# Float32r parts for every second channel's column transform in all batches, with more of the v product on ScalarE

## The chip, the cores and the metric

The kernel runs on one core of a Trainium2 chip. The metric is the device time of one execution in microseconds (us). The kernel before takes 3088.14 us, the median of three runs (3085.73 to 3089.94). Five engines work side by side, each through its own queue in order: TensorE (PE; its weight loads are listed as PEld), VectorE (DVE), ScalarE (ACT), GpSimd (POOL) and SyncE (SP, which here only issues transfers). [...]

## The reference, cut to what matters

The input `x` has 4 batches of 64 channels of 256 x 256 float32. Four layers follow each other.

Layers 0, 1 and 3 are long convolutions. A small network of sines makes two filters of 256 values per channel, `hx` and `hy`; the two-dimensional filter is their outer product, so that the convolution separates into one along the rows and one along the columns. The reference does it with an FFT of twice the length and adds `x * bias`:

```python
y = irfft2(rfft2(x, s=(512, 512)) * rfft2(k, s=(512, 512)) / 512)[..., :256, :256]
out = y + x * bias[:, None, None]
```

Layer 2 works in a Haar wavelet basis:

```python
f1 = haar2d(x)
for i in range(2):
    f4 = einsum('bchw,oc->bohw', f1 * v[i], conv_w[i])
    acc += sign(f4) * relu(abs(f4) - tau[i])
y = haar2d(acc, inverse=True)
return y + x
```

The channels are mixed by a 64 x 64 matrix per coefficient place; `v` and `tau` depend on the place alone, so the kernel mixes first and multiplies by `v` afterwards.

## The kernel before, in words

**Filters.** The networks of the three convolution layers run first, on small tiles. Their filters go to DRAM (`pads`) padded with zeros, and `toeplitz` (line 158) reads a filter back as a 128 x 256 Toeplitz tile per axis. The products of `v` and of `tau` with fixed factors go to DRAM as `scales`, `GT` groups to a tile.

**Convolutions, forward part.** `convolutions(b, ticks, in_parts)` takes the 64 channels of one batch through five stages, one tick apart: `load` (x and a Toeplitz tile), `first` and `second` of layer 0, `first` and `second` of layer 1. Each of the four products is a `contract` (lines 167 and 168): for each half of the columns a product of 256 columns and one of 128. ACT copies the result of a `first` out of PSUM (`a`, L176); DVE evicts a `second` with `y = res * bias + product` (L189). The last stage, `pairs`, also does the first Haar level along the rows into a ring `sd` of 8 channels (L230, L231) and stores it to `keep`. Every four channels `levels` does the other row levels on DVE (L240, L241).

Then `down` does the Haar transform along the columns, one product of the 128 x 128 Haar matrix with 512 columns. It has two forms. The plain one (L263) multiplies float32 by float32. The other, used where `in_parts` is set, has `split` ahead of it: ACT rounds the tile to float32r (`w[:, 0]`, L251), DVE forms the remainder (`w[:, 1]`, L252), and `down` adds two float32r products in PSUM (L259). Before the change only batch 0 goes in parts. ACT copies the coefficients out (`co`, L267) and SP stores them to `coef` in DRAM.

**Mixing.** `mixing(b, start, n_act)` takes 64 groups, each 4 coefficient rows of all 64 channels. `load` brings a group's coefficients, and at every `GT`-th group a tile `vt` of scales. `mix` multiplies by the mixing matrix: four products of 256 columns into `px` (L308), a PSUM tile of two banks with two buffers. The product with `v` is shared: DVE does the first `16 - n_act` of 16 slices of 64 in one instruction (L325), ACT does the other `n_act` with one instruction each (L327), into the tile `f4`. In the order of the queues L327 stands behind L325's semaphore. `shrink` forms |f4| on ACT (L333) and its sign on ACT (L334), and DVE takes tau off (L335); `signed` multiplies (L340) and `add` sums the two terms into the result `z` in SBUF (L344). `n_act` is 8 in batches 0 to 2 and 6 in the last one.

**Inverse and the last convolution.** `inverse(b)` takes each channel of `z` through the inverse transforms (`pw`, L368 and L369; `pu`, L381), adds the residual, and goes on with layer 3 (`first`, `second` and the store). In batches 0 to 2 every third channel is put off: it is stored to `late`, and `convolution` does its layer 3 during the last batch's mixing.

**What sets the order.** Each stage is registered as an event with a tick and a place in the tick (`at`, `stream`), and the sorted list of events is the program's order. Channels of batch b + 1 are spread over the ticks in which batch b is mixed, some 0.8 to 0.9 channels a tick. From this order the framework makes one instruction queue for each engine; it also moves instructions within some distance, so that neighbours on an engine can change places. Buffers come from tags with a fixed number of buffers: `in` (x and the put-off channels, 4), `toep` (5), `f4` (2, shared by the v products, the inverse's parts and the split's parts), `vt` (2), and four PSUM banks `mm` for all products but `px`. A tile waits until the oldest tile of its tag has been read for the last time.

Of the kernel before, what the change touches and what calls it, by code (L numbers as in the profile page):

```python
# [9 lines left out]
F32 = mybir.dt.float32  # L10
F32R = mybir.dt.float32r
# [5 lines left out]
B, C, S, EMB, ORD = 4, 64, 256, 33, 64  # L17
P = 128
ROW = S + P

GT = 8
BUFS = {"res": 1, "y": 3, "co": 2}

INV_2PI = float(np.float32(1.0 / (2.0 * math.pi)))
# [13 lines left out]
def conv_seq_kernel(ctx, tc, x, fz, fw, bias, decay, haar, haar_row, factors, vt, taut, wmix, out):  # L38
# [37 lines left out]
    with tc.tile_pool(name="filt", bufs=2) as fp, tc.tile_pool(name="fps", bufs=4, space=PSUM) as fps:  # L76
# [12 lines left out]
        for layer in range(3):  # L89
            z = fp.tile([EMB, S + 2 * ORD], F32, name=f"z{layer}", tag="z", bufs=3)  # L90
            nc.sync.dma_start(z, fz[layer])
            w = fp.tile([ORD, 2, 3 * ORD + 4], F32, name=f"w{layer}", tag="w", bufs=3)
# [5 lines left out]
        for step in range(3):  # L98
            for layer, axis in both:
                z, w = zs[layer], ws[layer]  # L100
# [8 lines left out]
                u = fp.tile([ORD, S], F32, name=f"u{step}_{layer}_{axis}", tag="u", bufs=3)  # L109
# [102 lines left out]
                if stage is not None:  # L212
                    at(tick + s, -s, stage, unit)

    def convolutions(b, ticks, in_parts=False):

        st = {}

        def load(c):
            xt = io.tile([P, 2, S], F32, name=f"x_{b}_{c}", tag="in", bufs=4)  # L220
            nc.sync.dma_start(xt, x[b, c].rearrange("(k p) w -> p k w", p=P))
            st[c] = {"x": xt, 0: toeplitz(0, c, f"t0_{b}_{c}")}

        last_second = second(b, st, "a1", 1, "y0", "y1", "res")

        def pairs(c):
            last_second(c)
            v = st.pop(c)["y1"].rearrange("p k (w e) -> p k w e", e=2)
            t = sd[:, c % 8]
            nc.vector.tensor_add(t[:, :, 0, :], v[:, :, :, 0], v[:, :, :, 1])  # L230
            nc.vector.tensor_sub(t[:, :, 1, :], v[:, :, :, 0], v[:, :, :, 1])  # L231
            nc.scalar.dma_start(keep[b][c], t)

        def levels(steps):
            def run(n):
                t = sd[:, n % 2 * 4 : n % 2 * 4 + 4]
                for step in steps:
                    v = t[:, :, :, 0, :].rearrange("p c k (w e) -> p (c k) w e", e=2 * step)
                    even, odd = v[:, :, :, 0], v[:, :, :, step]
                    nc.vector.tensor_sub(odd, even, odd)  # L240
                    nc.vector.scalar_tensor_tensor(even, even, 2.0, odd, ALU.mult, ALU.subtract)  # L241

            return run

        parts = {}

        def split(c):

            w = parts[c] = mx.tile([P, 2, 2, S], F32R, name=f"sp_{b}_{c}", tag="f4")
            t = sd[:, c % 8].rearrange("p k e w -> p k (e w)")  # L250
            nc.scalar.copy(w[:, 0], t)  # L251
            nc.vector.tensor_tensor(w[:, 1], t, w[:, 0].bitcast(F32), ALU.subtract)  # L252

        def down(c):
            ps = bank(f"pz_{b}_{c}")
            flat = "p k w -> p (k w)"
            if in_parts:
                for i in range(2):
                    nc.tensor.matmul(  # L259
                        ps.rearrange(flat), hbr, parts[c][:, i].rearrange(flat), start=(i == 0), stop=(i == 1)  # L260
                    )
            else:
                nc.tensor.matmul(  # L263
                    ps.rearrange(flat), hbt, sd[:, c % 8].rearrange("p k e w -> p (k e w)"), start=True, stop=True
                )
            t = io.tile([P, 2, S], F32, name=f"co_{b}_{c}", tag="co", bufs=BUFS["co"])
            nc.scalar.copy(t, ps)  # L267
            nc.sync.dma_start(coef[b][:, c].rearrange("k p w -> p k w"), t)

        stream(  # L270
            [load, first(b, st, "x", 0, "a0"), second(b, st, "a0", 0, "x", "y0", "y", ahead=1), first(b, st, "y0", 1, "a1"), pairs],
            ticks,
        )
        for n in range(C // 4):
            end = ticks[4 * n + 3] + 4
            for s, steps in enumerate([(1,), (2, 4), (8, 16, 32, 64)]):
                at(end + 1 + s, 1, levels(steps), n)
            for j in range(4):
                if in_parts:
                    at(end + 3 + j, 2, split, 4 * n + j)  # L280
                at(end + 4 + j, 2, down, 4 * n + j)
        return ticks[-1] + 11

    def mixing(b, start, n_act):

        st = {}

        def load(g):
            f = mx.tile([P, 2, S], F32, name=f"f_{b}_{g}", tag="f", bufs=3)
            nc.sync.dma_start(f, coef[b].rearrange("k c p w -> (k c) p w")[:, 2 * g : 2 * g + 2])  # L290
            st[g] = {"f": f}
            if g % GT == 0:
                t = mx.tile([P, 2, GT, 16], F32, name=f"vt_{b}_{g}", tag="vt")
                nc.sync.dma_start(t, scales[g // GT])
                st["vt", g // GT] = t

        def scale(g, i):
            return st["vt", g // GT][:, i, g % GT, :]

        def over(g, i, n):  # L300
            return scale(g, i)[:, :n].unsqueeze(2).to_broadcast([P, n, C])

        def mix(g):
            f = st[g]["f"]
            ps = psx.tile([P, 2, 2, S], F32, name=f"px_{b}_{g}", tag="mix")
            for q in range(2):
                for h in range(2):
                    nc.tensor.matmul(  # L308
                        ps[:, h, q, :],
                        f[:, q, h * P : (h + 1) * P],  # L310
                        wb.rearrange("p r n -> p (r n)"),
                        start=True,
                        stop=True,
                    )
            if g == 0:

                one, two = ps[:, :, 0, :P], ps[:, :, 0, P:]
                d = mx.tile([P, 2, P], F32, name=f"d_{b}", tag="mag")
                nc.vector.tensor_copy(d, two)
                nc.vector.tensor_sub(two, one, d)  # L320
                nc.vector.tensor_add(one, one, d)
            f4 = mx.tile([P, 16, C], F32, name=f"f4_{b}_{g}", tag="f4")
            px = ps.rearrange("p h q (r i o) -> p (h q r i) o", r=2, i=2)
            n = 16 - n_act
            nc.vector.tensor_tensor(f4[:, :n], px[:, :n], over(g, 0, n), ALU.mult)  # L325
            for j in range(n, 16):
                nc.scalar.mul(f4[:, j], px[:, j], scale(g, 0)[:, j : j + 1])  # L327
            st[g]["f4"] = f4

        def shrink(g):  # L330
            f4 = st[g]["f4"]
            mag = mx.tile([P, 16, C], F32, name=f"mag_{b}_{g}", tag="mag")
            nc.scalar.activation(mag, f4, AF.Abs)  # L333
            nc.scalar.activation(f4, f4, AF.Sign)  # L334
            nc.vector.tensor_sub(mag, mag, over(g, 1, 16))  # L335
            st[g]["mag"] = mag

        def signed(g):
            mag = st[g]["mag"]
            nc.vector.scalar_tensor_tensor(mag, mag, 0.0, st[g]["f4"], ALU.max, ALU.mult)  # L340

        def add(g):
            parts = st.pop(g)["mag"].rearrange("p (h r i) o -> p h r i o", h=2, i=2)
            nc.vector.tensor_add(z[:, :, 4 * g : 4 * g + 4, :], parts[:, :, :, 0, :], parts[:, :, :, 1, :])  # L344

        for g in range(S // 4):
            at(start + g - 2, 0, load, g)
            for s, stage in enumerate([mix, shrink, signed, add]):
                at(start + g + s, -1 - s, stage, g)
# [61 lines left out]
    def convolution(which, ticks):  # L411

        for (b, c), tick in zip(which, ticks):
            st = {}

            def load(c, b=b, st=st):
                u = io.tile([P, 2, S], F32, name=f"v_{b}_{c}", tag="in", bufs=4)
                nc.sync.dma_start(u, late[b, c])
                st[c] = {"u": u, 2: toeplitz(2, c, f"t2_{b}_{c}")}

            for s, stage in enumerate([load, *last(b, st)]):
                at(tick + s, -s, stage, c)


    def spread(begin, end, n=C):
        return [begin + i * (end - begin - 1) // (n - 1) for i in range(n)]
# [1 line left out]

    put_off = range(2, C, 3)
    groups = S // 4  # L430
    ready = convolutions(0, range(C), in_parts=True)
    ahead = C
    start = ready + 3
    for b in range(B):
        mixing(b, start, 8 if b + 1 < B else 6)
        end = start + groups + 3
        if b + 1 < B:
            ready = convolutions(b + 1, spread(ahead, end + 2))
        else:
            convolution(  # L440
                [(i, c) for i in range(B - 1) for c in sorted(put_off)], spread(start - 2, end + 2, (B - 1) * len(put_off))
            )
        inverse(b, end, put_off if b + 1 < B else ())

        start = max(end + C, ready + 3)
        ahead = start - 3
# [112 lines left out]
```

## Time and profile before

| | before |
|---|---|
| time, median of 3 | 3088.14 us |
| span of the profiled execution | 3090.0 us |
| TensorE granted clock | 0.999 |
| HBM traffic | 209 GB/s over the span |

The share of busy time by slice (40 slices of 77 us; a digit is tenths, 9 is 90% or more) shows the stages. DVE and ACT are fuller where a batch is mixed, slices 6 to 11, 15 to 20, 24 to 29 and 33 to 36:

```profile
PE   5999999999999999999999999999999999999999
DVE  6667677999987878888886879888886889998776
ACT  1333336777765656667665656666774667887554
```

In the tables of groups the columns are the line, the engine and operation, what is written and read, the shapes and the number of instructions; then the busy time in us and the mean duration of one in ns; then how long the engine stood idle just before them and whom it waited for. Where instructions of a kind overlap at their ends, the busy time is less than the number times the mean. In the table of waits the columns are the waiting line, the line that released it, the total in us, how often, and the longest. A timeline row has the start, the length, the engine, the line, and how many instructions were merged into it. A float32 product shows as two instructions.

### The profile page before, as it was taken

How to read it: one execution, taken by the hardware profiler on the slowest of the kernel's cores; microseconds unless marked ns; L12 is line 12 of the kernel's file. 1: busy time of each engine (PE TensorE's matmuls, PEld its weight loads, DVE VectorE, ACT ScalarE, POOL GpSimd, SP SyncE). 2: the span in 40 equal slices, each digit the busy share in tenths (PEclk: the TensorE clock that was granted, in tenths of full speed). 3: DMA queues.
4: the chain of work that ended last, by engine and by line, in shares of the span. 5: the costliest groups of instructions: out<-in, count | busy, mean ns of one | idle time of the engine just before them, and what ended most of it. 6: DMA issues, size and time to landing. Idle time of an engine off the chain costs nothing. (4 is left out here: it accounts for less than half of the span.)

```text
span 3090.0 us, 50474 instructions
## 1 busy us (share of the span) xinstructions
PE 3004.4 (97%) x16944; PEld 2615.3 (85%) x16944; DVE 2523.4 (82%) x4453; ACT 1926.9 (62%) x4054; POOL 0.2 (0%) x4
## 2 busy tenths in 40 slices
PE   5999999999999999999999999999999999999999
PEld 3999988888888888888887888888887888888998
DVE  6667677999987878888886879888886889998776
ACT  1333336777765656667665656666774667887554
POOL 0000000000000000000000000000000000000000
PEclk9999999999999999999999999999999999999999
DMA  4777877666667876666667776666667777877676
GB/s 118 217 230 230 234 227 211 196 193 197 195 193 228 238 223 196 195 207 199 194 205 216 236 229 196 199 195 204 198 195 218 235 238 228 236 233 212 210 211 188
DMA packets 555573, 649.26 MB, mean 210 GB/s; under 512 B 39761, under 2 KB 440500, under 8 KB 555188
## 3 DMA queue, kind: packets, MB, share of 16 engines
q1 hardware_dynamic: 439316, 493.18, 56.5%
q10 hardware_dynamic: 116000, 152.87, 13.7%
q8 instruction: 136, 2.23, 0.3%
q14 instruction: 121, 0.99, 0.1%
HBM read 426.40 MB, written 219.48 MB: 209 GB/s over the span
## 5 line engine op out<-in xcount | busy, mean ns | idle before, releaser
L167 PE MATMUL py<-t,a 128*128 128x256 f32 x3072 | 926.0, 383 | 27.9 <-ACT a L176 24.6
L176 ACT COPY a<-pa 128x512 f32<-128x512 f32 x768 | 458.7, 597 | 466.3 <-PE pa L168 330.7
L168 PEld LDWEIGHTS py<-t,a 128*128 128x128 f32 x3072 | 584.1, 190 | 79.4
L327 ACT ACTIVATE f<-px,vt 128x64 f32<-128x64 f32 x1920 | 422.0, 329 | 352.7 <-DVE f L325 348.3
L167 PEld LDWEIGHTS py<-t,a 128*128 128x128 f32 x3072 | 488.4, 191 | 126.1 <-issue 63.2
L168 PE MATMUL py<-t,a 128*128 128x128 f32 x3072 | 590.6, 274 | 0.0
L308 PE MATMUL px<-wb,f 128*128 128x256 f32 x2048 | 494.2, 380 | 4.3 <-ACT f L327 4.3
L308 PEld LDWEIGHTS px<-wb,f 128*128 128x128 f32 x2048 | 366.0, 191 | 44.1 <-ACT f L327 6.7
L335 DVE TENSOR_TENSOR mag<-mag,vt 128x1024 f32<-128x1024 f32 x256 | 312.2, 1219 | 36.0 <-ACT mag L333 34.8
L167 PE MATMUL pa<-t,x 128*128 128x256 f32 x1024 | 307.5, 382 | 9.4 <-DMA t<-pad 9.3
L340 DVE SCALAR_TENSOR_TENSOR mag<-mag,f 128x1024 f32<-128x1024 f32 x256 | 311.4, 1216 | 0.3
L167 PE MATMUL pa<-t,y 128*128 128x256 f32 x1024 | 306.3, 381 | 1.2 <-DVE y L189 0.9
L333 ACT ACTIVATE mag<-f 128x1024 f32<-128x1024 f32 x256 | 283.9, 1109 | 12.6 <-DVE z L344 6.8
L361 ACT COPY zc<-z 128x512 f32<-128x512 f32 x256 | 281.9, 1102 | 3.9 <-DVE z L199 2.6
L371 ACT CAST w<-pw 128x512 fp32r<-128x512 f32 x256 | 150.2, 587 | 212.3 <-PE pw L369 201.3
L334 ACT ACTIVATE f<-f 128x1024 f32<-128x1024 f32 x256 | 272.0, 1062 | 9.7 <-DVE sd L231 2.4
L189 DVE SCALAR_TENSOR_TENSOR y<-y,bsb,py 128x512 f32<-128x512 f32 x256 | 190.1, 743 | 104.5 <-PE py L168 103.7
L385 DVE SCALAR_TENSOR_TENSOR t<-r,pu 128x512 f32<-128x512 f32 x256 | 175.3, 685 | 86.6 <-PE pu L381 79.6
L189 DVE SCALAR_TENSOR_TENSOR y<-x,bsb,py 128x512 f32<-128x512 f32 x256 | 190.1, 743 | 62.6 <-PE py L168 54.0
L167 PE MATMUL pa<-t,u 128*128 128x256 f32 x772 | 234.1, 385 | 1.1 <-DVE y L189 0.7
L189 DVE SCALAR_TENSOR_TENSOR y<-u,bsb,py 128x512 f32<-128x512 f32 x193 | 143.8, 745 | 102.4 <-PE py L168 98.7
L168 PEld LDWEIGHTS pa<-t,x 128*128 128x128 f32 x1024 | 195.7, 191 | 26.9
(65 smaller groups left out, 4370.7 us busy)
## 6 DMA issues: line engine op xcount, KB each, us to landing
t<-pad SPq DMA_DIRECT2D x768, 256.0 KB, 3.9
x<-in_x SPq DMA_DIRECT2D x256, 256.0 KB, 3.9
keep<-sd ACTq DMA_DIRECT2D x256, 256.0 KB, 3.3
coef<-co SPq DMA_DIRECT2D x256, 256.0 KB, 3.1
f<-coef SPq DMA_DIRECT2D x256, 256.0 KB, 3.9
r<-keep SPq DMA_DIRECT2D x256, 256.0 KB, 3.4
out_y<-y ACTq DMA_DIRECT2D x256, 256.0 KB, 3.6
late<-u ACTq DMA_DIRECT2D x63, 256.0 KB, 2.6
```

What stands on the lines that cost most here:

```text
L167: nc.tensor.matmul(ps[:, m, :], src[:, 0, m * P : (m + 1) * P], t[:, ::-1], start=True, stop=False)
L168: nc.tensor.matmul(ps[:, m, P:], src[:, 1, m * P : (m + 1) * P], t[:, : P - 1 : -1], start=False, stop=True)
L176: nc.scalar.copy(a, ps)
L189: nc.vector.scalar_tensor_tensor(y, s[res], bsb[:, layer, c : c + 1], ps, ALU.mult, ALU.add)
L308: nc.tensor.matmul(ps[:, h, q, :], f[:, q, h * P : (h + 1) * P], wb.rearrange("p r n -> p (r n)"), start=True, stop=True,)
L327: nc.scalar.mul(f4[:, j], px[:, j], scale(g, 0)[:, j : j + 1])
L333: nc.scalar.activation(mag, f4, AF.Abs)
L334: nc.scalar.activation(f4, f4, AF.Sign)
L335: nc.vector.tensor_sub(mag, mag, over(g, 1, 16))
L340: nc.vector.scalar_tensor_tensor(mag, mag, 0.0, st[g]["f4"], ALU.max, ALU.mult)
L361: nc.scalar.copy(a, z[:, :, :, c].rearrange("p h (i k) -> p h k i", k=2))
L385: nc.vector.scalar_tensor_tensor(t, st[c]["r"], 0.5, ps, ALU.mult, ALU.add)
```

## The change

It does three things together, and makes room for them.

- `down` in two float32r parts for every even channel of batches 1 to 3, as well as for all channels of batch 0. It is for PE[...]. `in_parts` becomes the set of channels.
- In the mixings of batches 0 to 2 ACT takes 12 of the 16 slices of the v product (8 before), DVE 4. It is for DVE, which has the remainders to form.
- The parts get a tag of their own, `sp`, with one buffer of 4 KB per partition, where they used the two buffers of `f4`, which the mixing needs.
- For the room, `in` goes from 4 to 3 buffers (2 KB less), and `GT` from 8 to 4 groups per tile of scales (1 KB less; twice as many loads of half the size).

```diff
-GT = 8
+GT = 4
...
-    def convolutions(b, ticks, in_parts=False):
+    def convolutions(b, ticks, in_parts=()):
...
-            xt = io.tile([P, 2, S], F32, name=f"x_{b}_{c}", tag="in", bufs=4)
+            xt = io.tile([P, 2, S], F32, name=f"x_{b}_{c}", tag="in", bufs=3)
...
-            w = parts[c] = mx.tile([P, 2, 2, S], F32R, name=f"sp_{b}_{c}", tag="f4")
+            w = parts[c] = mx.tile([P, 2, 2, S], F32R, name=f"sp_{b}_{c}", tag="sp", bufs=1)
...
-            if in_parts:
+            if c in in_parts:
                 for i in range(2):
                     nc.tensor.matmul(
                         ps.rearrange(flat), hbr, parts[c][:, i].rearrange(flat), start=(i == 0), stop=(i == 1)
...
-                if in_parts:
+                if 4 * n + j in in_parts:
                     at(end + 3 + j, 2, split, 4 * n + j)
...
-                u = io.tile([P, 2, S], F32, name=f"v_{b}_{c}", tag="in", bufs=4)
+                u = io.tile([P, 2, S], F32, name=f"v_{b}_{c}", tag="in", bufs=3)
...
-    ready = convolutions(0, range(C), in_parts=True)
+    ready = convolutions(0, range(C), in_parts=range(C))
...
-        mixing(b, start, 8 if b + 1 < B else 6)
+        mixing(b, start, 12 if b + 1 < B else 6)
...
-            ready = convolutions(b + 1, spread(ahead, end + 2))
+            ready = convolutions(b + 1, spread(ahead, end + 2), in_parts=range(0, C, 2))
```

## The prediction

> **What bounds the kernel now.** I read the page first: busy shares, then each engine's share by time.
>
> ```profile
> span 3090.0 us, 50474 instructions
> PE 3004.4 (97%) x16944; PEld 2615.3 (85%) x16944; DVE 2523.4 (82%) x4453; ACT 1926.9 (62%) x4054; POOL 0.2 (0%) x4
> ```
>
> TensorE (PE) leads, but a kernel with stages is read stage by stage. The three mixings that the change touches run from the first to the last `px` product: 479.7 to 901.3, 1142.3 to 1601.4, 1848.5 to 2309.4 us. The fourth, 2552.3 to 2825.4, keeps its 6 products on ScalarE (ACT). The table of stretches gives them in another order, after the two middle ones:
>
> ```profile
> 1142.30:1601.40 459.10, 452.71 (x2429) 389.67 (x2428) 403.50 (x669) 317.12 (x793) 0.00 (x0) 1.00 0.67 199
> 1848.50:2309.40 460.90, 454.15 (x2430) 390.05 (x2429) 403.43 (x669) 316.97 (x793) 0.00 (x0) 1.00 0.67 198
> 479.70:901.30 421.60, 414.60 (x2178) 352.95 (x2177) 382.26 (x628) 308.40 (x777) 0.00 (x0) 1.00 0.65 195
> 2552.30:2825.40 273.10, 268.10 (x1435) 235.62 (x1435) 265.31 (x310) 233.97 (x553) 0.00 (x0) 1.00 0.79 231
> ```
>
> Columns: length, busy PE, PEld, DVE, ACT, POOL, clock, DMA. One group takes length/63: 7.29, 7.32, 6.69 and 4.33 us. In the second mixing PE is busy 98.6%, VectorE (DVE) 88%, ACT 69%. The fourth shows PE at 98% beside DVE at 97% and ACT at 86%, so neighbours that full need not slow PE.
>
> PE's own work must be counted from start-to-start times, because ends are modelled. The timeline of PE around one `down` of each kind:
>
> ```profile
> 1306.74 0.38 PE L168 MATMUL pa<-t,x 128*128 128x128 f32 x2
> 1306.96 1.02 PE L263 MATMUL pz<-sd,hbt 128*128 128x512 f32 x2
> 1307.82 0.59 PE L167 MATMUL py<-t,a 128*128 128x256 f32 x2
> ```
> ```profile
> 203.43 0.39 PE L168 MATMUL pa<-t,x 128*128 128x128 f32 x2
> 203.56 0.71 PE L259 MATMUL pz<-sp,hbr 128*128 128x512 f32 x2
> 204.11 0.59 PE L167 MATMUL py<-t,a 128*128 128x256 f32 x2
> ```
>
> From the preceding L168 to the following L167 is 1.08 us with the float32 `down`, 0.68 us with the parts: 0.40 us apart. The first form alone occupies 0.86 us (1306.96 to 1307.82), so the second counts 0.46. In the same way a `contract` takes 1.31 us (two L167 and two L168 rows, 1305.65 to 1306.96) and a group's `px` 1.73 us (1303.92 to 1305.65). In the second mixing 57 channels x 4 contracts x 1.31 + 49 downs x 0.86 + 63 x 1.73 = 299 + 42 + 109 = 450 us of 459; in the first (49 channels) 257 + 42 + 109 = 408 of 422. So PE is short of its own sum by 2 to 3% there. What takes that is the hand-over between ACT and DVE; ACT's waits in 1142 to 1602 us:
>
> ```profile
> ACT f L327 <- DVE f L325: 115.7, 57, 3.5
> ACT a L176 <- PE py L168: 8.6, 4, 4.2
> ```
>
> ACT stands 115.7 us behind DVE's share of the product. Per group there is a loop: Abs (L333, ACT), minus tau (L335, DVE), often a y eviction (L189) and the shrink product (L340), then DVE's v product (L325), ACT's v products (L327), copies, Abs of the next group. With start-to-start times 1.17, 1.16, 0.68 x 48/63, 1.16 x 41/63, 0.68, 8 x 0.20 = 1.60 plus one to two copies of 0.47 it is about as long as PE's tick. Following both queues row by row with such times gives 6.7 and 7.3 us a group, the 6.69 and 7.29 measured. Two limits lie close together: PE at 6.5 and 7.1 us, the loop at 6.7 and 7.3.
>
> [...] 8 products run in 1.75 us, 0.20 to start-to-start. [...] the trace has 684 and, for the 256-column copy out of `px` (L319), 417.
>
> **The change part by part.** The rows used:
>
> ```profile
> L327 ACT ACTIVATE f<-px,vt 128x64 f32<-128x64 f32 x1920 | 422.0, 329 | 352.7 <-DVE f L325 348.3 <-DMA keep<-sd 4.1
> L263 PE MATMUL pz<-sd,hbt 128*128 128x512 f32 x384 | 197.7, 597 | 9.1 <-DVE sd L241 7.7 <-DVE w L372 1.4
> L325 DVE TENSOR_TENSOR f<-px,vt 128x512 f32<-128x512 f32 x192 | 131.2, 684 | 1.2
> L252 DVE TENSOR_TENSOR sp<-sd,sp 128x512 fp32r<-128x512 f32 x64 | 44.1, 689 | 57.5 <-ACT sp L251 56.0 <-PE py L168 1.4
> L251 ACT CAST sp<-sd 128x512 fp32r<-128x512 f32 x64 | 40.3, 631 | 2.2 <-DVE sd L241 2.2
> ```
>
> PE: 3 batches x 32 channels leave the float32 form, 96 x 0.40 = 38.4 us less. Of these about 73 lie in mixings (half of the 49 downs in each), 29.4 us; 23 lie in the stretches between, 9.0 us.
>
> ACT: 192 groups x 4 more products x 0.20 = +154 us, and 96 split copies x 0.47 (start to start, as L176) = +45 us. Per group +0.80 and +0.18: in the second mixing from 317/63 = 5.03 to 6.0 us of a tick near 7.1, 85%.
>
> DVE: L325 falls from 512 to 256 columns, 684 to about 417 ns (bounds 0.36, its start-to-start, and 0.42): 192 x 0.27 = -51 us. The 96 subtractions add 96 x 0.63 = +60 us. DVE stays at 6.4 us a group, 90%.
>
> The loop: the products add 0.80, L325 gives back 0.26. With the old order of the queues that would be +0.54 a group. But the instruction order of the changed kernel differs: DVE's next v product stands ahead of the shrink product in 42 of 63 pairs (22 before) in the second and third mixing, in 58 (43) in the first; the y eviction stands between L335 and L325 in 29 (48) and 15 (35). That takes 0.37 + 0.21 off in the second mixing, 0.28 + 0.22 in the first: the tally is level, -0.04 and +0.04. Copies that move into ACT's wait take off more: the row-by-row sum gives 6.55 and 7.2 us, 0.15 and 0.10 less than before. I take this, below PE's 29.4: 63 x (0.15 + 0.10 + 0.10) = 22 us.
>
> The split ahead of a `down`: at the end of each of three conversions PE waited 2 to 3.4 us in L263 for the Haar levels (L241). There the two halves now follow the levels, 0.6 + 0.6 us, 3 times: +3.6 us. Elsewhere the split runs a tick ahead, hidden by the other four contracts.
>
> `sp` gets one own buffer instead of two of `f4`. In batch 0 the split of channel c+1 then follows the `down` of c in ACT's queue, behind the copy L267 that waits for the same product: no new wait, and the result is due a tick (5.7 us) later. Cost zero, hidden by the contracts.
>
> `in` with 3 buffers: x loads of batch 0 go out as the fourth last is freed, 15 to 16 us before use; v loads of the last mixing 11.5 to 15 us before. One buffer less takes one tick, 5.7 and 4.3 us. At least 7 us stay for a landing of 3.9 to 4.1 us: zero, unless DVE lags. `GT` 4: 32 more loads of half the size on SP, two ticks ahead; zero.
>
> Sum: -22 - 9.0 + 3.6 = -27, so 3061 us.
>
> **The rivals.**
> 1. PE gets all of it: 3088 - 38 = 3050 us. For it: PE 98% busy, DVE and ACT both fuller in the fourth mixing. Against it: the loop explains the measured period better than PE's sum.
> 2. Slower: PE's queue stalls at `px`. In the changed order 81 groups' `px` wait for ACT to free the bank (57 before), some directly behind the previous `px`, with the contracts queued behind. The wait before was 0.8 us at most and 4.3 in all; a whole block of products is 12 x 0.20 = 2.4. With 24 (the added ones) to 63 (all that lie in the three mixings) stalls of 1.2 us, half a block, +29 to +76 on 3061: 3090 to 3137. If the loop rose by the +0.54 of the old order in place of falling, 189 x 0.54 - 5 = +97, 3185. For it: ACT's spare time in a group falls from 2.2 to 1.1 us while its waits persist. Against it: the fourth mixing.
> 3. No change: mixings stay pinned by the loop, only the stretches between gain, 3088 - 9 + 3.6 = 3083 us.
>
> **How the numbers follow.** Forecast (3053 to 3072) 0.45, rival 1 (below) 0.15, rival 3 and its neighbourhood (3072 to 3094) 0.22, rival 2 (beyond) 0.18. Range 3045 to 3094: below it lies more than PE can give, above it rival 2. Within 0.2% (3082 to 3094) 0.12; faster 0.45 + 0.15 + 0.10 = 0.70; slower 0.18.
>
> **What would show it.** Right: L263 x192 and L259 x320 instructions; groups in the three mixings near 6.55 and 7.2 us; ACT near 2120 us in all, DVE near 2530; ACT still waiting on L325, but under 1.2 us a group; the fourth mixing unchanged at 273 us. Wrong: `px` waiting for L327 by tens of us, `pa` waiting for loads of x or v, or the loop longer because L334 now stands behind the first product of the next group (8 to 20 of 63 pairs, 1 or none before), so that ACT idles through L335 and L325.

## The result, and the profile after

The changed kernel takes 3049.98 us (median of 4 runs, 3042.65 to 3052.63) against 3086.93 us for the kernel before in the same comparison: ratio 0.9877, 95% interval 0.9857 to 0.9897. That is 37 us less, where 27 were forecast. The time, 3050 us, lies just below the forecast's 3053 to 3072 and is that of rival 1.

The page of the changed kernel, busy shares:

```profile
span 3050.6 us, 51749 instructions
PE 2971.9 (97%) x16944; PEld 2615.0 (86%) x16944; DVE 2518.7 (83%) x4549; ACT 2117.0 (69%) x4918; POOL 0.2 (0%) x4
```

TensorE (PE) lost 32.5 us of modelled busy time, VectorE (DVE) is level (2519, 2530 forecast) and ScalarE (ACT) went from 1927 to 2117 (2120 forecast). The added loads of the engines are as worked out. The stretches from the first to the last `px`, columns as before:

```profile
481.10:890.50 409.40, 403.51 (x2180) 350.55 (x2179) 375.81 (x650) 367.04 (x1052) 0.00 (x0) 1.00 0.67 202
1131.80:1577.80 446.00, 443.42 (x2421) 388.13 (x2420) 395.59 (x690) 373.90 (x1068) 0.00 (x0) 1.00 0.68 204
1823.20:2268.80 445.60, 443.42 (x2421) 388.16 (x2420) 395.56 (x690) 373.95 (x1068) 0.00 (x0) 1.00 0.68 204
2513.60:2785.90 272.30, 267.69 (x1436) 235.73 (x1435) 265.20 (x310) 233.95 (x553) 0.00 (x0) 1.00 0.79 232
```

| stretch | before | after | difference |
|---|---|---|---|
| mixing 1 | 421.6 | 409.4 | -12.2 |
| mixing 2 | 459.1 | 446.0 | -13.1 |
| mixing 3 | 460.9 | 445.6 | -15.3 |
| mixing 4 | 273.1 | 272.3 | -0.8 |
| between 1 and 2, 2 and 3, 3 and 4 | 241.0, 247.1, 242.9 | 241.3, 245.4, 244.8 | +0.3, -1.7, +1.9 |

So the three mixings gave 40.6 us, and the stretches between them nothing. The stretches do not hold quite the same work: in the second and third mixing one `contract` of PE has moved behind the last `px` (2421 PE instructions where there were 2429 and 2430). With its 1.31 us put back, the mixings gave 38.0 us and the stretches between them 2.1. A group takes 6.50, 7.08 and 7.07 us. Of the 40.6 us, 31.1 are PE's busy time (1321.5 to 1290.4 in the three; 2.6 of it are the two contracts) and 9.5 are PE idle time (20.1 to 10.7). In the second mixing of the changed kernel ACT waits for this:

```profile
ACT f L327 <- DVE f L325: 34.8, 32, 4.5
ACT a L176 <- PE pa L168: 26.1, 12, 2.7
```

Its wait for DVE's share of the product fell from 115.7 us to 34.8, while its busy time rose from 317 to 374. Idle time of ACT was filled; what that was worth by itself, the experiments show. Rows of the changed kernel's groups:

```profile
L327 ACT ACTIVATE f<-px,vt 128x64 f32<-128x64 f32 x2688 | 585.0, 348 | 103.2 <-DVE f L325 102.7
...
L259 PE MATMUL pz<-sp,hbr 128*128 128x512 f32 x320 | 116.1, 442 | 9.5 <-ACT sp L251 9.5
...
L252 DVE TENSOR_TENSOR sp<-sd,sp 128x512 fp32r<-128x512 f32 x160 | 109.8, 686 | 68.2 <-ACT sp L251 68.2
...
L325 DVE TENSOR_TENSOR f<-px,vt 128x256 f32<-128x256 f32 x192 | 80.4, 419 | 5.8 <-PE px L308 5.3
```

L325 with 256 columns takes 419 ns (417 taken), L252 686 ns, and the 768 added products cost 163 us of busy time (154 estimated).

### The profile page after: what moved, and what is told of

Same layout as the page of the kernel before. It is cut to its first block, busy times and chain, and to the rows that moved or that the text cites. A ratio compares the mean times of both kernels' runs of the same rounds, so it can differ in the third digit from the quotient of the medians.

```text
span 3050.6 us, 51749 instructions
## 1 busy us (share of the span) xinstructions
PE 2971.9 (97%) x16944; PEld 2615.0 (86%) x16944; DVE 2518.7 (83%) x4549; ACT 2117.0 (69%) x4918; POOL 0.2 (0%) x4
## 5 line engine op out<-in xcount | busy, mean ns | idle before, releaser
L167 PE MATMUL py<-t,a 128*128 128x256 f32 x3072 | 924.5, 383 | 16.6 <-ACT a L176 11.1
L176 ACT COPY a<-pa 128x512 f32<-128x512 f32 x768 | 475.5, 621 | 464.5 <-PE pa L168 352.9
L327 ACT ACTIVATE f<-px,vt 128x64 f32<-128x64 f32 x2688 | 585.0, 348 | 103.2 <-DVE f L325 102.7
L168 PEld LDWEIGHTS py<-t,a 128*128 128x128 f32 x3072 | 584.0, 190 | 79.5
L168 PE MATMUL py<-t,a 128*128 128x128 f32 x3072 | 590.5, 274 | 0.0
L167 PEld LDWEIGHTS py<-t,a 128*128 128x128 f32 x3072 | 491.0, 191 | 89.7 <-issue 32.8
L335 DVE TENSOR_TENSOR mag<-mag,vt 128x1024 f32<-128x1024 f32 x256 | 312.5, 1221 | 52.8 <-ACT mag L333 51.8
L167 PE MATMUL pa<-t,x 128*128 128x256 f32 x1024 | 307.5, 382 | 9.8 <-DMA t<-pad 9.8
L340 DVE SCALAR_TENSOR_TENSOR mag<-mag,f 128x1024 f32<-128x1024 f32 x256 | 312.0, 1219 | 1.1
L167 PE MATMUL pa<-t,y 128*128 128x256 f32 x1024 | 306.6, 381 | 1.3 <-DVE y L189 1.1
L334 ACT ACTIVATE f<-f 128x1024 f32<-128x1024 f32 x256 | 278.7, 1088 | 27.0 <-DVE sd L231 15.6
L167 PE MATMUL pa<-t,u 128*128 128x256 f32 x772 | 236.2, 388 | 2.1 <-DVE u L389 1.4
L168 PEld LDWEIGHTS pa<-t,x 128*128 128x128 f32 x1024 | 195.7, 191 | 26.8
```

What stands on the lines that cost most here:

```text
L167: nc.tensor.matmul(ps[:, m, :], src[:, 0, m * P : (m + 1) * P], t[:, ::-1], start=True, stop=False)
L168: nc.tensor.matmul(ps[:, m, P:], src[:, 1, m * P : (m + 1) * P], t[:, : P - 1 : -1], start=False, stop=True)
L176: nc.scalar.copy(a, ps)
```

## The experiments

Each ratio is to the kernel before on the same chip. That kernel took 3092.65 us beside the first four runs, 3087.53 beside the second four and 3089.60 beside the third, so across the tables ratios are compared, not medians. "Mixings" is the sum of the three stretches in that run's profile (before: 1341.6 us).

### First: which of the parts does it

All start from the changed kernel. `e1_room` and `e2_products` undo the parts, `e1_room` and `e3_parts` undo the products, `e4_all` extends the parts.

```diff
 # e1_room, e2_products
-            ready = convolutions(b + 1, spread(ahead, end + 2), in_parts=range(0, C, 2))
+            ready = convolutions(b + 1, spread(ahead, end + 2), in_parts=())
 # e1_room, e3_parts
-        mixing(b, start, 12 if b + 1 < B else 6)
+        mixing(b, start, 8 if b + 1 < B else 6)
 # e4_all
-            ready = convolutions(b + 1, spread(ahead, end + 2), in_parts=range(0, C, 2))
+            ready = convolutions(b + 1, spread(ahead, end + 2), in_parts=range(C))
```

Expected of `e1_room`:

> The changed kernel with both of its main parts undone: no channel of batches 1 to 3 in parts, 8 products on ScalarE; what is left is the room (sp with one buffer, in with 3, GT 4). Both theories: no change, 3087 within 6 us. A rival in which the smaller load buffers delay loads: 3095 or more, with waits of pa for x or v.

Expected of `e2_products`:

> The room and the 12 products on ScalarE, without parts in batches 1 to 3. If the hand-over between ScalarE and VectorE set the pace of the mixings, a shorter share of VectorE shortens it: 15 to 25 us faster, 3062 to 3072. If TensorE's own work sets it: at most the 9 to 13 us a mixing that TensorE was short of its sum can shrink a little, 3075 to 3087. If 12 products are too many for ScalarE: slower than 3093.

Expected of `e3_parts`:

> The room and every second channel in parts, with 8 products on ScalarE as before. If TensorE's work sets the pace: most of the 38 us, 3050 to 3060, since VectorE rises only to 6.65 us of a tick of 7.0. If the hand-over sets it: the remainders (0.63 us each on VectorE) lengthen it, and no more than 10 us come back, 3077 to 3095.

Expected of `e4_all`:

> As the changed kernel, with all channels of batches 1 to 3 in parts. TensorE theory: 96 more channels at 0.40 us, up to 38 us below the changed kernel, 3012, less what ScalarE (6.2 us a group) and VectorE (6.65) take at a tick of 6.9: 3012 to 3035. Hand-over theory: no further gain, 3045 to 3060; if VectorE at 96 per cent of the tick chokes it, slower than the changed kernel.

| run | median us | ratio, interval | mixings |
|---|---|---|---|
| `e1_room` | 3092.94 | 1.0008 (1.0000 to 1.0016) | 1340.9 |
| `e2_products` | 3086.07 | 0.9980 (0.9973 to 0.9986) | 1333.8 |
| `e3_parts` | 3051.84 | 0.9872 (0.9859 to 0.9886) | 1305.0 |
| `e4_all` | 3039.29 | 0.9833 (0.9820 to 0.9847) | 1289.8 |

The parts alone bring all of it: 1.28% with 8 products, as much as the whole change with 12 (1.23%). The products alone bring 0.20% (0.28% against `e1_room`, which has the same room), or 6 to 9 us where the hand-over theory had 15 to 25. The room costs 0.16% at most. Between `e1_room` and `e3_parts` lie 41 us, or 0.43 us for each of the 96 channels (the intervals leave 0.05 to either side), where the timeline of before gave 0.40. PE's idle time in the three mixings is 20.0 us in `e1_room`, 13.0 in `e2_products`, 14.1 in `e3_parts` and 10.7 in the changed kernel: each part takes some of PE's waits away by itself, and together they take little more. The three mixings of `e3_parts`:

```profile
479.90:889.60 409.70, 403.42 (x2180) 351.96 (x2179) 389.67 (x647) 321.53 (x801) 0.00 (x0) 1.00 0.67 201
1131.00:1580.00 449.00, 444.40 (x2430) 389.52 (x2429) 414.94 (x693) 327.27 (x819) 0.00 (x0) 1.00 0.68 204
1825.50:2271.80 446.30, 443.08 (x2429) 389.32 (x2428) 414.80 (x693) 327.41 (x819) 0.00 (x0) 1.00 0.68 205
```

This run speaks against the hand-over as the bound. DVE's queue stands almost as before (its next v product is ahead of the shrink product in 23 of 63 pairs of the second mixing, 22 before; the y eviction is between in 48, as before), its share of products is that of before, and it got more work: 93% of the three mixings. ACT's queue did change: between an Abs and the first product of the next group lie 91 copies in the second mixing, where 53 lay before (80 and 40 in the first), 24 of them the new copies of the splits. The row-by-row sum for these queues, worked out as in the prediction (an estimate), is 6.7 and 7.2 us a group: nothing less than before in the first mixing, 0.1 less in the second. The chip came down by 0.2 in both, to 6.50, 7.13 and 7.08, which is what PE's 0.40 us per channel promise (about 25 channels x 0.40 / 63 = 0.16) and a little more. From here to the changed kernel the sum falls by 0.15 in the first mixing, to 6.55, and there the chip does not follow: 6.50 in both. The sum does not foretell the pace. No run takes work off PE and leaves both other queues as they were.

The second half of the channels (`e4_all`) brought 12 to 14 us more, not 38; the time lies between what the two theories gave. The largest wait of PE in that run:

```profile
PE px L308 <- ACT f L327: 20.3, 32, 1.2
```

### Second: repeated products, and other shares of the work

`e8_repeat` is `e3_parts` with repeated products:

```diff
                 nc.scalar.mul(f4[:, j], px[:, j], scale(g, 0)[:, j : j + 1])
+            if b + 1 < B:
+                for j in range(12, 16):
+                    nc.scalar.mul(f4[:, j], px[:, j], scale(g, 0)[:, j : j + 1])
```

The other three are `e4_all` with one edit each:

```diff
 # e9_all_ten, and with 8 in place of 10 e11_all_eight
-        mixing(b, start, 12 if b + 1 < B else 6)
+        mixing(b, start, 10 if b + 1 < B else 6)
 # e10_pool
-            nc.vector.tensor_tensor(w[:, 1], t, w[:, 0].bitcast(F32), ALU.subtract)
+            (nc.gpsimd if b else nc.vector).tensor_tensor(w[:, 1], t, w[:, 0].bitcast(F32), ALU.subtract)
```

Expected of `e8_repeat`:

> The kernel with parts for even channels and 8 products on ScalarE, in which ScalarE forms 4 of its 8 products a second time in the mixings of batches 0 to 2 (the same values again): 0.80 us more in each group's hand-over and nothing given back by VectorE. TensorE theory: ScalarE rises to 6.0 us of a tick of 7.1 and the time stays within 10 us of the run without the repeats, 3048 to 3062. Hand-over theory: 189 x 0.80 = 151 us at most, and half of it if the order of the queues shifts, 3125 to 3200.

Expected of `e9_all_ten`:

> All channels in parts, 10 products on ScalarE. In the run with 12 TensorE waited 20 us at px for ScalarE, and VectorE was busy 92, ScalarE 88 per cent of the mixings. If ScalarE's block of products before px is freed is what cost the second half: 5 to 12 us below 3039. If it is VectorE, which rises to 95 per cent: 3040 to 3055.

Expected of `e10_pool`:

> All channels in parts, 12 products, and the remainders of batches 1 to 3 on GpSimd in place of VectorE, which is so relieved of 192 x 0.63 = 121 us. If VectorE took the second half of the gain: 3012 to 3030. If ScalarE did: 3032 to 3042. If GpSimd is too slow for a remainder in a tick of 6.9 us, or slows VectorE beside it: slower than 3045.

Expected of `e11_all_eight`:

> All channels in parts with 8 products on ScalarE, as before the change. VectorE then needs 1203 + 189 x 0.27 = 1254 us of some 1290 in the three mixings, 97 per cent. If 97 per cent can be borne, as in the fourth mixing: about 3039, and the 12 products are worth nothing. If not: 3045 to 3070, and this is what the 12 products are for.

| run | median us | ratio, interval | mixings |
|---|---|---|---|
| `e8_repeat` | 3044.79 | 0.9863 (0.9847 to 0.9880) | 1296.9 |
| `e9_all_ten` | 3018.08 | 0.9771 (0.9756 to 0.9785) | 1272.9 |
| `e10_pool` | 3134.33 | 1.0149 (1.0134 to 1.0164) | 1370.8 |
| `e11_all_eight` | 3037.13 | 0.9835 (0.9821 to 0.9850) | 1291.1 |

The second mixing of `e8_repeat`:

```profile
1129.80:1573.10 443.30, 440.70 (x2421) 388.08 (x2420) 409.39 (x689) 375.66 (x1067) 0.00 (x0) 1.00 0.68 205
```

ACT carries 0.77 us more in each group there (375.66 us for 327.27 in `e3_parts`), nothing is taken off DVE, and the time does not rise (0.9863 beside 0.9872, the intervals overlap). So ACT's work as such is not the bound. The longer hand-over that the run was meant to make did not come about, because the queues were made anew around the repeats: in the second mixing DVE's next v product is ahead of the shrink product in 48 of 63 pairs (23 in `e3_parts`), the y eviction between in 21 (48). At the start-to-start times of the prediction, 1.16 and 0.68 us, that takes an estimated 0.46 + 0.29 us off the loop, as much as the repeats add. Against the hand-over stand `e3_parts` and `e2_products`, not this run.

With all channels in parts 10 products are better than 8 and than 12 by 19 to 20 us. `e9_all_ten` is 69 us below the kernel before and 33 below the change; of the 2 x 38.4 = 77 us that 0.40 us per channel promise, it has nine tenths. The expectation for 10 was right in direction and too small (5 to 12 us). With 8 it came as expected if DVE at 96% can be borne (about 3039), so that 12 are worth no more than 8; that a number between them beats both was not foreseen.

GpSimd for the remainders failed. Two rows of that run's groups:

```profile
L252 POOL TENSOR_TENSOR sp<-sd,sp 128x512 fp32r<-128x512 f32 x192 | 273.4, 1424 | 2160.3 <-ACT sp L251 1673.9 <-DMA t<-pad 467.8 <-PE px L308 18.6
...
L230 DVE TENSOR_TENSOR sd<-y 128x256 f32<-128x256 f32 x256 | 127.0, 496 | 8.9 <-DVE y L189 1.4
```

A remainder takes 1424 ns there and 686 on DVE (the changed kernel), a factor of 2.1. Some of DVE's own instructions took longer as well: L230 496 ns, where it takes 422 in `e9_all_ten` (all channels in parts, remainders on DVE); L335 takes 1219 in both. PE waited 45.1 us at `px` and 21.3 us for y evictions (20.3 and 5.1 in `e4_all`). Whether that explains all of the 97 us against `e4_all` was not taken apart; the granted clock was also a little lower, 0.993 for 0.998.

### Third: the number of products, and the stretches between

```diff
 # e12_even_ten: the changed kernel with 10; e13_all_nine and e14_all_eleven: e9_all_ten with 9, 11
-        mixing(b, start, 12 if b + 1 < B else 6)
+        mixing(b, start, 10 if b + 1 < B else 6)
 # e15_ends_plain: e9_all_ten with
-            ready = convolutions(b + 1, spread(ahead, end + 2), in_parts=range(C))
+            ready = convolutions(b + 1, spread(ahead, end + 2), in_parts=range(C - 4))
```

Expected of `e12_even_ten`:

> The changed kernel with 10 products on ScalarE in place of 12. With all channels in parts 10 gave 21 us over 12 and over 8. If the number of products counts only where VectorE and ScalarE are near the tick (all channels in parts): within 6 us of the changed kernel, 3045 to 3056. If 12 is too many for ScalarE's block ahead of px here too: 3035 to 3045.

Expected of `e13_all_nine`:

> All channels in parts, 9 products. With 8 it was 3037, with 10 3018. If the load is what counts (VectorE 96 per cent): between them, 3024 to 3032. If the order of the queues, which shifts with each number, counts more: anywhere in 3010 to 3040.

Expected of `e14_all_eleven`:

> All channels in parts, 11 products. With 10 it was 3018, with 12 3039. By load alone (ScalarE 85 to 86 per cent): between them, 3024 to 3034. By the order of the queues: anywhere in 3010 to 3040.

Expected of `e15_ends_plain`:

> All channels in parts and 10 products, but the last four channels of batches 1 to 3 in one float32 product. TensorE waits for the levels there anyway, so that the parts save 12 x 0.40 = 5 us and put two halves of a split (1.2 us) ahead of three of the waits. If gains ahead of a wait end in the wait: the waits of pz for L251 vanish, those for L241 stay near 9 us, and the time is within 5 us of 3018. If TensorE's passes count there as elsewhere: 5 us slower, 3023.

| run | median us | ratio, interval | mixings |
|---|---|---|---|
| `e12_even_ten` | 3044.38 | 0.9852 (0.9838 to 0.9865) | 1298.4 |
| `e13_all_nine` | 3025.47 | 0.9788 (0.9775 to 0.9802) | 1281.9 |
| `e14_all_eleven` | 3021.74 | 0.9778 (0.9765 to 0.9791) | 1275.9 |
| `e15_ends_plain` | 3018.99 | 0.9768 (0.9755 to 0.9782) | 1276.1 |

With even channels in parts, 8, 10 and 12 products give 0.9872, 0.9852 and 0.9877, with overlapping intervals: 12 against 10 is worth 8 us at the centre and stays undecided. With all channels the number counts:

| products, all channels | 8 | 9 | 10 | 11 | 12 |
|---|---|---|---|---|---|
| ratio | 0.9835 | 0.9788 | 0.9771 | 0.9778 | 0.9833 |
| DVE busy in the mixings | 96.0% | 95.8% | 95.7% | 94.7% | 93.3% |
| ACT busy in the mixings | 78% | 82% | 86% | 88% | 89% |
| PE idle in the mixings, us | 23.9 | 17.5 | 10.1 | 9.6 | 24.1 |
| PE waits for ACT's `a` copies, whole kernel, us | 22.7 | 14.5 | 10.1 | 6.1 | 11.2 |
| PE waits for ACT's products at `px`, whole kernel, us | 4.3 | 4.3 | 6.1 | 6.8 | 20.3 |

9 products came near the lower edge of where the load alone puts them (3025 for 3024 to 3032, or 3022 by the ratio), 11 a little below it (3022 for 3024 to 3034, or 3019). At 8 and at 12 PE's idle time in the mixings is 14 us longer than at 10, most of the 19 to 20 us lost, and the two ends lose by different waits: at 8, PE waits for copies; at 12, for the PSUM tile that the products hold. The step from 11 to 12 is 17 us, while ACT goes from 88% to 89% of the mixings and DVE falls; that the load alone makes it is hard to see, but is not excluded. The order of the queues jumps as well: in the first mixing the first ACT product of the next group stands ahead of the sign in 38 of 63 pairs with 12, 29 with 11, 19 with 10. Whether the load or the order makes the step, no run separates.

`e15_ends_plain` has 12 channels fewer in parts than `e9_all_ten` and is as fast (0.9768, 0.9771). Its waits of PE at `pz`:

```profile
PE pz L263 <- DVE sd L241: 7.1, 3, 2.4
...
PE pz L259 <- DVE sp L252: 3.2, 6, 1.2
PE pz L259 <- ACT sp L251: 2.9, 2, 2.1
```

The wait for the Haar levels is back, three times of 2.4 us, as in the kernel before; in `e9_all_ten` PE waits three times for 2.9 us at this place, for the split. So parts gain nothing that can be measured at the last four channels of a batch: the 12 x 0.40 = 4.8 us that they promise do not show in the time, and some 1.6 us of them go into the longer wait. The intervals, 0.13% or 4 us to either side, would hide most of an effect of this size.

## Why the prediction was right, and where it was not

- *PE's 0.40 us per channel.* Right. From `e1_room` to `e3_parts` it is 0.43 us. The changed kernel shows the instructions forecast, 192 of L263 and 320 of L259, and in its second mixing the same times from the preceding L168 to the following L167, 1.08 us with the float32 `down` and 0.68 with the parts. Why the parts take PE less time, the traces do not show; only the times are measured.
- *"The loop ... I take this, below PE's 29.4: 22 us."* This is the step that failed. The mixings gave 40.6 us in place of 22. The row-by-row sum had given 6.7 and 7.3 us where the kernel before takes 6.69 and 7.29, and I took that agreement for a cause. It did not hold in a second case: from before to `e3_parts` the sum hardly moves while the chip gains 0.2 us a group, and from there to the changed kernel the first mixing's sum falls by 0.15 while the chip stands still. Nor was there reason to put all of PE's shortfall of 2 to 3% down to the loop: ACT's 115.7 us behind DVE are a wait of ACT, while PE's own waits in the same stretch of the kernel before are these two, 6.4 us:

```profile
PE py L167 <- ACT a L176: 5.5, 8, 1.0
PE pa L167 <- DMA t<-pad: 0.9, 1, 0.9
```

- *The added products and DVE's smaller share.* Sizes right (163 us for 154; 419 ns for 417), effect on the time close to none in this change: `e3_parts` without them is as fast.
- *9.0 us from the stretches between, and 3.6 us lost to the split.* Wrong in both terms. Together -5.4 us were forecast; the stretches grew by 0.5 us, or shrank by 2.1 without the two contracts that moved into them. Not 23 but 20 channels in parts lie there, which promise 8 us; PE's busy time in the three fell by only 1.0 us (714.5 to 713.5), or 3.6 without the contracts. The rest did not go into waits: PE's idle time there is 16.5 us before and 18.0 after, its waits at `pz` 9.1 (L263 for L241 and L372) and 9.5, so that the split's 3.6 us are not seen either. `e3_parts` shows the same: 1 us against `e1_room`. Why a channel in parts gives less there than in a mixing stays open.
- *Room at no cost.* Right: `e1_room`, 0.16% at most. No wait of `pa` for x or v appeared.
- *Rival 2, PE stuck at `px`.* It did not come: 6.8 us in the whole kernel, against 4.3. It is real further on, with 20.3 us in `e4_all`.

The waits at `px` and `pz` in the changed kernel:

```profile
PE pz L259 <- ACT sp L251: 9.5, 3, 3.7
...
PE px L308 <- ACT f L327: 6.8, 11, 1.1
```

That the sum came out only 10 us short (by the medians) is in part luck, because two errors partly cancelled. In the two profiles, with the two contracts put back, it had 16.0 us too little in the mixings (22 for 38.0) and 3.3 too much between them (5.4 for 2.1).

## What to carry to other kernels

A long wait of an engine that is not the bound can be idle time and no more (here ACT's 115.7 us behind DVE, beside 6.4 us of PE's own waits in the same stretch): ask whose waits the bounding engine has, and add those up, before a loop of two other engines is made a limit. A model that agrees with one measurement shows nothing until a second one, in which its inputs differ, agrees as well. A run that is to lengthen a loop must be looked at again after it is built: the framework may order the queues anew and take off what was added. Work saved on the bounding engine need not be worth the same in every stage: here a channel in parts was worth 0.40 us or more in the mixings and about 0.1 between them. Moving work between two helpers paid most once one of them was near the tick (0.64% from 8 to 10 products with all channels in parts, 0.28% from 8 to 12 with none).

## What the runs showed that was not expected

- The best version found is all channels in parts with 10 products: 3018 us, ratio 0.9771, against 0.9877 for the change.
- In the mixings of `e9_all_ten` PE is busy 99.2%, DVE 95.7% and ACT 85.8% of the same 1273 us, although each waits for the others in its queue:

```profile
sum 1272.90, PE 1262.79 PEld 1129.59 DVE 1218.17 ACT 1091.93 POOL 0.00; mean PE 420.93 PEld 376.53 DVE 406.06 ACT 363.98 POOL 0.00
```

- ACT absorbed 0.77 us more a group, from 5.2 to 6.0 us of 7.0, with no cost (`e8_repeat`).
- The remainders on GpSimd cost twice: 1424 ns for one of 512 columns where DVE takes 686, and in the same run DVE's L230 took 496 ns where it takes 422 in `e9_all_ten`, 17% more.
